# Four chunks of a spiking layer in turn, and two other stages step by step with them: the order of one hybrid kernel's front part

## The chip, the cores and the metric

The kernel runs on one NeuronCore of a Trainium2 chip. The metric is the device time of one execution in microseconds (us); the time before is the median of three runs. All engines of the core work side by side, each in the order of its own instruction stream: TensorE (PE, matrix products and transposes), VectorE (DVE), ScalarE (ACT, activation functions), GpSimd (POOL) and SyncE (SP, which here issues DMAs). An instruction waits on semaphores for what other engines produce, and everything behind it on the same engine waits with it.

## The reference

The input x has two batches of 1024 rows of 128 features, in float32. Seven blocks add to it in turn, each on a layer norm of x. The change touches how the first five are put in order:

```python
x = x + latent_attention(layernorm(x))        # 16 heads, softmax
x = x + spiking_ffn(layernorm(x))
x = x + state_space(layernorm(x))             # projections, then a scan over time
x = x + spiking_ffn(layernorm(x))
x = x + linear_attention(layernorm(x))        # a norm of its own inside
x = x + experts(layernorm(x))                 # 8 experts, summed
x = x + attention_over_batches(layernorm(x))
x = x + experts(layernorm(x))
```

with the spiking layer

```python
h = square(relu(x @ W_fc.T))                  # 128 -> 512
y = h @ W_proj.T                              # 512 -> 128
out = number_of_spikes_in_5_steps(y) / 5
```

The number of spikes grows with y, so it is computed as a count of five thresholds that y reaches.

## The kernel before

x stays on the chip as `x_res`, 16 tiles of 128 rows. A batch is 8 tiles, a *chunk* 4 tiles (512 rows), so a batch has two chunks, and chunks 0 and 1 are batch 0, 2 and 3 batch 1.

The blocks depend on each other only within a batch (until the attention over batches), so the kernel puts a part of one batch beside a part of the other. Each part is a Python generator that issues some instructions and yields: one *step*. `weave(main, side, rate)` takes a step of `main`, then as many of `side` as the rate has come due, until `main` ends; `drain` takes what is left. All of this stands in `first_layer` under a manual schedule of every engine: each engine executes in just the order in which the program issues. So the order of steps is the order of every queue. These are its stages from there on, after latent attention of batch 0:

| stage | main | side | rate |
|---|---|---|---|
| A | `into_space(0)`: spiking layer, then state space prologue, batch 0 | `row_maxima(1)` of latent attention, batch 1 | 1.25 |
| loop 0 | state space loop, batch 0 | `attend(1)`, the rest of latent attention | 1.75 |
| B | `out_of_space(0)`: second spiking layer, then linear attention, batch 0 | `into_space(1)` | 1.2 |
| loop 1 | state space loop, batch 1 | `expert_steps`, batch 0 | 1.4 |
| C | `out_of_space(1)` | the rest of `expert_steps` | 0.6 |

*The spiking layer* (`spiking_steps`) takes its chunks one after the other, in 9 steps each: statistics of the norm on DVE (L60, L61; a pair for each tile) and their root on ACT (L64); inverse and norm on DVE (L67, L71, four instructions for `f_u`); four transposes on PE (L94, `f_pt`) and a copy on ACT (L411, `f_uT`); four steps of a product (L416, `f_ph`), Relu (L418) and Square (L419) on ACT; the output product on PE (L424, `f_py`, 32 passes); and on DVE the count (L433, four times L436) and the sum into `x_res` (L439).

*The prologue* of the state space (22 steps) computes statistics and two roots, normalizes (L514, `s_u` on DVE; L517, `s_un` on ACT), transposes (L521, `s_pt`), and multiplies by the norm's weight (L522, `s_xnT`). Then come the projections, all by line 485 (`s_pm`): the input projection with the convolution, whose Silu on ACT gives `s_xc`; `wd1T`, which DVE copies to `s_rT`; the skip gates; and for each half of the features and each chunk a chain `s_z` (L555, DVE), Abs, Exp and Ln on ACT (L556 to L559), and DVE again to `s_delta` (L565) and `s_dtx` (L566). SP writes these out for the loop to load.

*Linear attention* (`linear_steps`, 13 steps) normalizes twice, `l_u` and `l_un`, each with statistics, root and eight instructions of L71 on DVE; transposes (`l_pt`, L94; `l_xnT`, L689); projects keys (`l_pm`, L695) with a maximum and an exponential, values (`l_pv`, L716) and, after transposing the keys (`l_pkt`, L725), the queries (`l_pm` again); then forms the context (`l_pc`, L734), applies it (`l_pa`, L744) and projects out (`l_po`, L750).

*Row maxima* has 49 steps: a step makes the scores of up to 512 keys for the heads of one group on PE (L223; L232 adds the mask), into three buffers `a_s`, and DVE reduces them (L241, two instructions, `a_nm`). *An expert step* (65 in all) issues two products (L799 and L800), a Silu on ACT (L802), a product on DVE (L804, `e_h`), and the output product of the step before (L823, `e_po`), which thus waits for `e_h`: a *unit*.

In stage B, eight experts' weights are loaded by SP: `load_experts`, one load for each of the first eight steps of `out_of_space(0)`.

Of the kernel before, what the change touches and what calls it, by code (L numbers as in the profile page):

```python
# [9 lines left out]
F32 = mybir.dt.float32  # L10
BF16 = mybir.dt.bfloat16
AF = mybir.ActivationFunctionType
ALU = mybir.AluOpType
# [4 lines left out]
P = 128  # L18
B = 2
L = 1024  # L20
D = 128
# [54 lines left out]
def weave(main, side, rate):  # L76

    due = 0.0
    for _ in main:
        due += rate  # L80
        while due >= 1.0:
            next(side, None)
            due -= 1.0


def drain(steps):
    for _ in steps:
        pass


def transpose4(g, ps, src):

    for t in range(4):
        g.nc.tensor.transpose(ps[:, t, :], src[:, t, :], g.ident)  # L94
# [284 lines left out]
def _fires_from(count):  # L379

    low, high = (int(np.float32(v).view(np.int32)) for v in (0.0, 2.0))
    while high - low > 1:
        mid = (low + high) // 2
        if _spikes(np.int32(mid).view(np.float32)) >= count:
            high = mid
        else:
            low = mid
    return float(np.int32(high).view(np.float32))


SPIKES_AT = [_fires_from(count) for count in range(1, 6)]


def spiking_steps(g, w, chunks, work, bank):

    nc = g.nc
    FC = 4
    for n in chunks:
        xs = g.x[:, 4 * n : 4 * n + 4, :]
        u = work.tile([P, 4, D], F32, name="f0_u")  # L400
        ln = StagedNorm(g, xs, 4, "f0")
        ln.stats(range(4))
        ln.root()
        yield
        ln.inverse()
        ln.apply(u, range(4), nc.vector)
        yield
        pt = bank("f0_pt")
        transpose4(g, pt.rearrange("p (a b) -> p a b", a=4), u)
        uT = work.tile([P, 512], F32, name="f0_uT")  # L410
        nc.scalar.copy(uT, pt)  # L411
        yield
        hT = work.tile([P, FC, 512], F32, name="f0_hT")
        for fc in range(FC):
            ph = bank("f0_ph")
            nc.tensor.matmul(ph, w["wfcT"][:, bass.ts(fc, P)], uT, start=True, stop=True)  # L416
            r = work.tile([P, 512], F32, name="f0_r", bufs=2)
            nc.scalar.activation(r, ph, AF.Relu)  # L418
            nc.scalar.activation(hT[:, fc, :], r, AF.Square)  # L419
            yield  # L420
        py = bank("f0_py")
        for t in range(4):
            for fc in range(FC):
                nc.tensor.matmul(  # L424
                    py[:, bass.ts(t, P)],
                    hT[:, fc, bass.ts(t, P)],
                    w["wprojT"][:, fc, :],
                    start=(fc == 0),
                    stop=(fc == FC - 1),
                )  # L430
        yield
        cnt = work.tile([P, 512], F32, name="f0_cnt", bufs=2)
        nc.vector.tensor_scalar(cnt, py, SPIKES_AT[0], None, ALU.is_ge)  # L433
        for level in SPIKES_AT[1:]:
            c2 = work.tile([P, 512], F32, name="f0_cnt", bufs=2)
            nc.vector.scalar_tensor_tensor(c2, py, level, cnt, ALU.is_ge, ALU.add)  # L436
            cnt = c2
        xf = xs.rearrange("p a b -> p (a b)")
        nc.vector.scalar_tensor_tensor(xf, cnt, 1.0 / 5.0, xf, ALU.mult, ALU.add)  # L439
        yield  # L440

# [391 lines left out]
class ExpertStream:  # L835
# [3 lines left out]
    NE, FC = 8, 4  # L839
# [351 lines left out]
def first_layer(g, w, open_experts, load_expert):  # L1191

    tc = g.tc

    def pool(stack, name, bufs, **kw):
        return stack.enter_context(tc.tile_pool(name=name, bufs=bufs, **kw))

    def banks(stack, name, bufs, **kw):
        ps = pool(stack, name, bufs, space=PSUM, **kw)
        return lambda tile_: ps.tile([P, 512], F32, name=tile_, tag=name)  # L1200

    right = dict(side="right")
    ends, latents, spaces = ExitStack(), ExitStack(), ExitStack()
    latent = LatentAttention(g, w, pool(latents, "a0_keep", 1, **right))
    own = pool(latents, "a0_batch1", 1, **right)
    with ExitStack() as es:
        latent.project([pool(es, "a0_batch0", 1), own])
        with tc.tile_pool(name="a0_seq", bufs=1) as seq, tc.tile_pool(name="a0_ps_a", bufs=2, space=PSUM) as ps:
            drain(latent.row_maxima(0, seq, ps, 4))
        work = pool(es, "a0_work", 2)  # L1210
        ps, ps_o = pool(es, "a0_ps_b", 3, space=PSUM), pool(es, "a0_ps_o", 1, space=PSUM)
        drain(latent.attend(0, work, ps, ps_o))

    bank = banks(spaces, "bank", 2)
    shared = StateConstants(g, w, pool(spaces, "s_one", 1))
    seq = pool(spaces, "s_seq", 2)
    dram = pool(spaces, "s_dram", 2, space=bass.MemoryType.DRAM)
    space = [StateSpace(g, w, b, shared, seq, dram) for b in range(B)]

    def into_space(b, bank, **side):  # L1220

        with tc.tile_pool(name=f"f{b}_work", bufs=1, **side) as work:
            yield from spiking_steps(g, w, [2 * b, 2 * b + 1], work, bank)
        with tc.tile_pool(name=f"s{b}_work", bufs=1, **side) as work:
            yield from space[b].prologue(work, bank)

    def out_of_space(b, bank, each_step=iter(()), **side):

        with tc.tile_pool(name=f"f{b}_work", bufs=1, **side) as work:
            for _ in spiking_steps(g, w, [2 * b, 2 * b + 1], work, bank):  # L1230
                next(each_step, None)
                yield
        with tc.tile_pool(name="l_seq", bufs=1, **side) as work:
            yield from linear_steps(g, w, b, work, bank)

    def load_experts():
        for e in range(8):
            load_expert(e)
            yield

    with tc.manual_schedule(engines=ALL):
        with (
            tc.tile_pool(name="a0_seq", bufs=1, **right) as aseq,
            tc.tile_pool(name="a0_ps_a", bufs=3, space=PSUM, **right) as ps,
        ):
            maxima = latent.row_maxima(1, aseq, ps, 2)
            weave(into_space(0, bank), maxima, 1.25)
            drain(maxima)
        work = pool(latents, "a0_work", 1, **right)
        ps, ps_o = pool(latents, "a0_ps_b", 2, space=PSUM, **right), pool(latents, "a0_ps_o", 1, space=PSUM, **right)  # L1250
        attend = latent.attend(1, work, ps, ps_o)
        with tc.tile_pool(name="s_work", bufs=1, reuse_waits="tile") as work:
            weave(space[0].loop(work, bank), attend, 1.75)
        drain(attend)
        latents.close()
        open_experts()
        with ExitStack() as es:
            bank0, bank1 = banks(es, "bank0", 3, **right), banks(es, "bank1", 3, **right)
            side = into_space(1, bank1, **right)
            weave(out_of_space(0, bank0, load_experts()), side, 1.2)  # L1260
            drain(side)
        ework = pool(ends, "e_work", 2, **right)
        ps_e, ps_o = pool(ends, "e_ps", 2, space=PSUM, **right), pool(ends, "e_ps_o", 1, space=PSUM, **right)
        experts = expert_steps(g, w, [0, 1], ework, ps_e, ps_o)
        with tc.tile_pool(name="s_work", bufs=1, reuse_waits="tile") as work:
            weave(space[1].loop(work, bank), experts, 1.4)
        spaces.close()
        with ends, ExitStack() as es:
            weave(out_of_space(1, banks(es, "bank", 3)), experts, 0.6)
            drain(experts)  # L1270


# [1 line left out]
def kernel(ctx: ExitStack, tc: tile.TileContext, d: dict, out: bass.AP):  # L1274
# [30 lines left out]
    def load_expert(e):  # L1305
        for name in ("Wg", "Wu"):
            nc.sync.dma_start(out=w[name][:, e, :], in_=d[name][e])
        nc.sync.dma_start(out=w["Wd"][:, e], in_=d["Wd"][e].rearrange("(c p) o -> p c o", p=P))

    first_layer(g, w, open_experts, load_expert)  # L1310
    layer0.close()
    experts_ffn(g, w, [2])
# [70 lines left out]
```

## Time and profile before

| what | value |
|---|---|
| median of three runs | 2337.7 us (2337.57 to 2339.66) |
| the profiled execution | 2339.02 us, its span 2337.3 us |
| PE busy | 2024.7 us, 87% of the span, 15152 instructions |
| DVE busy | 1632.9 us, 70% |
| ACT busy | 1186.0 us, 51% |
| POOL busy | 1057.0 us, 45% |
| mean granted clock of PE | 0.937 |

The stages in the profiled execution, in us from the span's start:

| stage | from | to | length |
|---|---|---|---|
| projections and latent attention of batch 0 | 0 | 312.0 | 312.0 |
| A | 312.0 | 484.3 | 172.3 |
| loop 0 | 484.3 | 691.0 | 206.7 |
| B | 691.0 | 838.6 | 147.6 |
| loop 1 | 838.6 | 1046.9 | 208.3 |
| C | 1046.9 | 1145.6 | 98.7 |
| experts, attention over batches, experts | 1145.6 | 2337.3 | 1191.7 |

How to read the profile: a line of a timeline has the start and the busy time of a group of equal instructions, the engine, the line, the operation, the tile that it writes and those that it reads, and how many; in brackets the idle time of the engine ahead of it, and whose result ended that. A line of the chain of waits has start, length, engine, tile and line. The granted clock (PEclk) is a share of full speed.

### The profile page before, as it was taken

What the parts mean: (1) busy time and instruction counts of PE and PEld (TensorE: products, weight loads), DVE (VectorE), ACT (ScalarE), POOL (GpSimd) and SP (SyncE); (2) the same over time, 40 slices, a digit from 0 to 9 for tenths busy, and PEclk for the clock granted to TensorE, in tenths of its full rate; (3) what the DMA queues carried; (4) which work ended last, traced back from release to release, by engine and by line L of the source; (5) the groups of instructions that cost most, each with busy time, mean ns of one, the idle gap of its engine ahead of it and who ended that gap; (6) DMA issues with size and microseconds to landing.
All of it is one profiled execution on the core that took longest, in us unless ns stands there. A gap on an engine that the chain in (4) does not pass through costs nothing.

```text
span 2337.3 us, 36191 instructions
## 1 busy us (share of the span) xinstructions
PE 2024.7 (87%) x15152; PEld 1189.1 (51%) x15152; DVE 1632.9 (70%) x1988; ACT 1186.0 (51%) x1488; POOL 1057.0 (45%) x588
## 2 busy tenths in 40 slices
PE   7679988887986848788898898999977999999999
PEld 4223344223334413234446576777745777777764
DVE  5941057788874569984423798989977989898832
ACT  1024521254633468754322676777734777677722
POOL 0011100042310000100102599999999999999910
PEclk9989988878988879999899999999999999999999
DMA  3000000086741068630000000000000000000000
GB/s 86 1 1 1 1 1 1 18 205 155 179 111 55 19 163 189 158 83 0 1 1 1 1 1 2 1 2 1 2 6 1 2 2 1 2 6 1 2 5 5
DMA packets 35779, 85.92 MB, mean 37 GB/s; under 512 B 4960, under 2 KB 15648, under 8 KB 35488
## 3 DMA queue, kind: packets, MB, share of 16 engines
q1 hardware_dynamic: 35152, 82.28, 14.4%
q8 instruction: 119, 1.95, 0.4%
q10 hardware_dynamic: 464, 1.33, 0.3%
q14 instruction: 44, 0.36, 0.1%
HBM read 78.35 MB, written 5.24 MB: 36 GB/s over the span
## 4 chain that ended last, share of the span: by engine, by line
PE 41%; POOL 13%; DVE 10%; issue 3%; ACT 3%; DMA 1%; SPq 0%; DVEq 0%; ACTq 0%; POOLq 0%
PE h_pd L1062 7%; POOL h_a L1072 7%; PE e_pgu L877 6%; POOL h_e L1056 5%; PE h_pd L903 4%; PE h_s L1028 4%; PE e_pg L799 4%; PE h_po L1078 4%; PE e_po L823 4%; PE e_pu L800 3%; DVE s_h L636 2%; PE s_pm L485 1%; DVE e_h L804 1%; DVE s_h L635 1%; DVE h_m L1039 1%
## 5 line engine op out<-in xcount | busy, mean ns | idle before, releaser
L1072 POOL TENSOR_TENSOR h_a<-h_e,h_r 128x2048 f32<-128x2048 f32 x128 | 581.2, 4541 | 0.0
L1039 DVE TENSOR_REDUCE h_m<-h_s 128x128 f32<-128x2048 f32 x128 | 293.3, 2291 | 74.8 <-PE h_s L1028 74.6
L1056 POOL TENSOR_TENSOR h_e<-h_e 128x512 f32<-128x512 f32 x256 | 318.4, 1261 | 46.8 <-ACT h_e L1048 46.8
L1062 PE MATMUL h_pd<-h_e,ident 128*128 128x128 f32 x2048 | 279.7, 291 | 44.0 <-POOL h_e L1056 33.0
L1062 PEld LDWEIGHTS h_pd<-h_e,ident 128*128 128x128 f32 x2048 | 253.3, 200 | 96.9 <-POOL h_e L1056 77.4
L1048 ACT ACTIVATE h_e<-h_e 128x1024 f32<-128x1024 f32 x256 | 256.6, 1049 | 81.7 <-DVE h_e L1045 80.6
L1045 DVE TENSOR_TENSOR h_e<-h_s,h_m 128x2048 f32<-128x2048 f32 x128 | 292.6, 2286 | 2.7
L302 POOL TENSOR_SCALAR_AFFINE_SELECT a_pT<-a_pT 128x256 f32<-128x256 f32 x128 | 97.2, 774 | 428.6 <-ACT a_pT L299 427.7
L299 ACT ACTIVATE a_pT<-a_st 128x1024 f32<-128x1024 f32 (+1 forms) x192 | 145.2, 808 | 140.4 <-PE a_st L289 138.3
L884 ACT ACT_TABLE_LOAD x106 | 136.0, 1283 | 153.0 <-PE e_pgu L877 152.3
L804 DVE TENSOR_TENSOR e_h<-e_sg,e_pu 128x512 f32<-128x512 f32 x128 | 86.9, 685 | 177.0 <-PE e_pu L800 151.7
L241 DVE TENSOR_REDUCE a_nm<-a_s 128x2 f32<-128x1024 f32 (+7 forms) x144 | 168.1, 1218 | 44.4 <-PE a_s L232 24.0
L823 PE MATMUL e_po<-e_h,Wd 128*128 128x512 f32 x256 | 138.6, 627 | 40.4 <-DVE e_h L804 40.2
L802 ACT ACTIVATE e_sg<-e_pg 128x512 f32<-128x512 f32 x128 | 76.0, 596 | 189.7 <-PE e_pg L799 189.4
L903 PEld LDWEIGHTS h_pd<-Wd,e_h 128*128 128x128 f32 x1024 | 125.6, 191 | 90.5 <-DVE e_h L892 79.8
L223 PE MATMUL a_s<-a_latT,a_qT 32*128 32x512 f32 (+3 forms) x768 | 121.0, 606 | 53.6 <-DVE a_nm L241 52.0
L877 PE MATMUL e_pgu<-e_uT,Wg 128*128 128x256 f32 x512 | 154.3, 383 | 4.0 <-ACT h_qz L992 2.1
L903 PE MATMUL h_pd<-Wd,e_h 128*128 128x128 f32 x1024 | 149.2, 288 | 5.8 <-DVE e_h L892 3.6
L1028 PE MATMUL h_s<-h_qz,h_kT 32*128 32x512 f32 x1024 | 147.0, 644 | 8.1 <-DVE h_e L1045 7.0
L877 PE MATMUL e_pgu<-e_uT,Wu 128*128 128x256 f32 x512 | 152.4, 379 | 0.0
L636 DVE TENSOR_TENSOR_SCAN s_h<-s_a,s_h 128x1024 f32<-128x1024 f32 x64 | 147.3, 2302 | 5.9 <-ACT s_a L604 1.6
L1048 ACT ACT_TABLE_LOAD x107 | 137.3, 1283 | 26.0 <-DVE h_e L1045 21.0
(246 smaller groups left out, 3190.2 us busy)
## 6 DMA issues: line engine op xcount, KB each, us to landing
s_a<-s_steps SPq DMA_DIRECT2D x64, 512.0 KB, 4.8
s_h<-s_steps SPq DMA_DIRECT2D x64, 512.0 KB, 6.4
s_steps<-s_delta SPq DMA_DIRECT2D x4, 512.0 KB, 2.6
s_steps<-s_dtx SPq DMA_DIRECT2D x4, 512.0 KB, 3.3
Wg<-in_Wg_dram SPq DMA_DIRECT2D x8, 256.0 KB, 6.0
Wu<-in_Wu_dram SPq DMA_DIRECT2D x8, 256.0 KB, 5.9
Wd<-in_Wd_dram SPq DMA_DIRECT2D x8, 256.0 KB, 6.1
x_res<-in_x_dram SPq DMA_DIRECT2D x4, 256.0 KB, 7.9
```

The lines of the kernel that those rows point to most:

```text
L241: nc.vector.tensor_reduce(nm[:, half, i, h : h + together], s[:, :, :n], AX.X, ALU.max, negate=True)
L636: nc.vector.tensor_tensor_scan(h, a, h, 0.0, ALU.mult, ALU.add)
L823: nc.tensor.matmul(po, w["Wd"][:, e, fc, :], hp, start=(e == 0 and fc == 0), stop=last)
L877: nc.tensor.matmul(pgu[:, k, :], w[name][:, e, f], uT, start=True, stop=True)
L903: nc.tensor.matmul(po[:, t, :], h[:, bass.ts(t, P)], self.w["Wd"][:, e, fc, :], start=(k == 0), stop=(k == 1))
L1028: nc.tensor.matmul(s[:, j, :].rearrange("p (k q) -> p k q", k=K), kTs[b][quad, bass.ts(kb, P)], qzs[b][quad, :, bass.ts(qb, P)], start=Tru ...
L1039: nc.vector.tensor_reduce(m, heads.rearrange("p h q -> p q h"), AX.X, ALU.max)
L1045: nc.vector.tensor_sub(e, heads, m.unsqueeze(1).to_broadcast([P, H, P]))
L1048: nc.scalar.activation(eh, eh, AF.Exp, scale=scale)
L1056: nc.gpsimd.tensor_add(e2[:, 4 * half : 4 * half + 4, :], e[:, h0 : h0 + 4, :], e[:, h0 + 4 : h0 + 8, :])
L1062: nc.tensor.matmul(pd, g.ident, e2[:, k, :], start=(k == 0), stop=(k == 7))
L1072: nc.gpsimd.tensor_mul(a, e, r.unsqueeze(1).to_broadcast([P, H, P]))
```

## The change

`spiking_steps` takes one chunk instead of a list, with buffers that are named for the chunk's parity, and `merge` takes a step of each of several streams in turn. The two chunks of a batch's spiking layer become two streams that alternate, in `into_space` and `out_of_space` alike, so these have 9 rounds for it in place of 18 steps (31 and 22 steps in all, before 40 and 31). In stage B, `into_space(1)` and `out_of_space(0)` alternate too, in place of the weave at 1.2: so the four chunks go step by step in turn, and then a step of the prologue of batch 1 and a step of linear attention of batch 0, until linear attention ends. The rates in A and C become 1.6 and 0.8. Relu writes into `f0_hT` and Square works in place.

```diff
+def merge(*streams):
+    streams = list(streams)
+    done = object()
+    while streams:
+        streams = [stream for stream in streams if next(stream, done) is not done]
+        if streams:
+            yield
...
-def spiking_steps(g, w, chunks, work, bank):
+def spiking_steps(g, w, n, work, bank):
     nc = g.nc
     FC = 4
-    for n in chunks:
-        xs = g.x[:, 4 * n : 4 * n + 4, :]
-        u = work.tile([P, 4, D], F32, name="f0_u")
-        ln = StagedNorm(g, xs, 4, "f0")
...
-        uT = work.tile([P, 512], F32, name="f0_uT")
...
-        hT = work.tile([P, FC, 512], F32, name="f0_hT")
...
-            r = work.tile([P, 512], F32, name="f0_r", bufs=2)
-            nc.scalar.activation(r, ph, AF.Relu)
-            nc.scalar.activation(hT[:, fc, :], r, AF.Square)
...
-            c2 = work.tile([P, 512], F32, name="f0_cnt", bufs=2)
+    tile_ = lambda name, tag: work.tile([P, 512], F32, name=name, tag=f"{tag}{n % 2}")
+    xs = g.x[:, 4 * n : 4 * n + 4, :]
+    u = tile_("f0_u", "f0_a").rearrange("p (a b) -> p a b", a=4)
+    ln = StagedNorm(g, xs, 4, f"f{n}")
...
+    uT = tile_("f0_uT", "f0_b")
...
+    hT = work.tile([P, FC, 512], F32, name=f"f0_hT{n % 2}")
...
+        nc.scalar.activation(hT[:, fc, :], ph, AF.Relu)
+        nc.scalar.activation(hT[:, fc, :], hT[:, fc, :], AF.Square)
...
+        c2 = tile_("f0_cnt", "f0_a" if k % 2 else "f0_b")
...
 def into_space(b, bank, **side):
-            yield from spiking_steps(g, w, [2 * b, 2 * b + 1], work, bank)
+            yield from merge(*[spiking_steps(g, w, n, work, bank) for n in (2 * b, 2 * b + 1)])
...
 def out_of_space(b, bank, each_step=iter(()), **side):
-            for _ in spiking_steps(g, w, [2 * b, 2 * b + 1], work, bank):
+            for _ in merge(*[spiking_steps(g, w, n, work, bank) for n in (2 * b, 2 * b + 1)]):
                 next(each_step, None)
                 yield
...
-            weave(into_space(0, bank), maxima, 1.25)
+            weave(into_space(0, bank), maxima, 1.6)
...
-            side = into_space(1, bank1, **right)
-            weave(out_of_space(0, bank0, load_experts()), side, 1.2)
-            drain(side)
+            drain(merge(into_space(1, bank1, **right), out_of_space(0, bank0, load_experts())))
...
-            weave(out_of_space(1, banks(es, "bank", 3)), experts, 0.6)
+            weave(out_of_space(1, banks(es, "bank", 3)), experts, 0.8)
```

More of the change, by code (lines that the diff above doesn't have):

```diff
@@ L391 @@
 SPIKES_AT = [_fires_from(count) for count in range(1, 6)]
-def spiking_steps(g, w, chunks, work, bank):
+def spiking_steps(g, w, n, work, bank):
     nc = g.nc
     FC = 4
-    for n in chunks:
-        xs = g.x[:, 4 * n : 4 * n + 4, :]
-        u = work.tile([P, 4, D], F32, name="f0_u")
-        ln = StagedNorm(g, xs, 4, "f0")
-        ln.stats(range(4))
-        ln.root()
-        yield
[L405 to L409, printed above, removed]
-        uT = work.tile([P, 512], F32, name="f0_uT")
-        nc.scalar.copy(uT, pt)
-        yield
-        hT = work.tile([P, FC, 512], F32, name="f0_hT")
-        for fc in range(FC):
-            ph = bank("f0_ph")
-            nc.tensor.matmul(ph, w["wfcT"][:, bass.ts(fc, P)], uT, start=True, stop=True)
-            r = work.tile([P, 512], F32, name="f0_r", bufs=2)
-            nc.scalar.activation(r, ph, AF.Relu)
-            nc.scalar.activation(hT[:, fc, :], r, AF.Square)
[L420 to L434, printed above, removed]
-            c2 = work.tile([P, 512], F32, name="f0_cnt", bufs=2)
[L436 to L440, printed above, removed]
@@ new lines, in spiking_steps @@
+    tile_ = lambda name, tag: work.tile([P, 512], F32, name=name, tag=f"{tag}{n % 2}")
+    xs = g.x[:, 4 * n : 4 * n + 4, :]
+    u = tile_("f0_u", "f0_a").rearrange("p (a b) -> p a b", a=4)
+    ln = StagedNorm(g, xs, 4, f"f{n}")
+    ln.stats(range(4))
+    ln.root()
+    yield
+    ln.inverse()
+    ln.apply(u, range(4), nc.vector)
+    yield
+    pt = bank("f0_pt")
+    transpose4(g, pt.rearrange("p (a b) -> p a b", a=4), u)
+    uT = tile_("f0_uT", "f0_b")
+    nc.scalar.copy(uT, pt)
+    yield
@@ new lines, in spiking_steps @@
+    hT = work.tile([P, FC, 512], F32, name=f"f0_hT{n % 2}")
+    for fc in range(FC):
+        ph = bank("f0_ph")
+        nc.tensor.matmul(ph, w["wfcT"][:, bass.ts(fc, P)], uT, start=True, stop=True)
+        nc.scalar.activation(hT[:, fc, :], ph, AF.Relu)
+        nc.scalar.activation(hT[:, fc, :], hT[:, fc, :], AF.Square)
+        yield
+    py = bank("f0_py")
+    for t in range(4):
+        for fc in range(FC):
+            nc.tensor.matmul(
+                py[:, bass.ts(t, P)],
+                hT[:, fc, bass.ts(t, P)],
+                w["wprojT"][:, fc, :],
+                start=(fc == 0),
+                stop=(fc == FC - 1),
+            )
@@ L451 @@
+    yield
+    cnt = tile_("f0_cnt", "f0_a")
+    nc.vector.tensor_scalar(cnt, py, SPIKES_AT[0], None, ALU.is_ge)
+    for k, level in enumerate(SPIKES_AT[1:]):
+        c2 = tile_("f0_cnt", "f0_a" if k % 2 else "f0_b")
+        nc.vector.scalar_tensor_tensor(c2, py, level, cnt, ALU.is_ge, ALU.add)
+        cnt = c2
+    xf = xs.rearrange("p a b -> p (a b)")
+    nc.vector.scalar_tensor_tensor(xf, cnt, 1.0 / 5.0, xf, ALU.mult, ALU.add)
+    yield
 class StateConstants:
```

## The prediction

> **What bounds the kernel now.** I read the table of windows first, cut at the borders of the stages: the change touches three stretches, and everything between and after them keeps its instructions.
>
> ```profile
> core 0: us, PE busy (x) PEld busy (x) DVE busy (x) ACT busy (x) POOL busy (x), PEclk, DMA share, GB/s
> 312.00:484.30 172.30, 146.29 (x722) 64.86 (x720) 127.03 (x199) 44.34 (x64) 3.24 (x2) 0.82 0.07 20
> 691.00:838.60 147.60, 95.80 (x376) 54.74 (x368) 75.64 (x206) 61.29 (x98) 7.33 (x4) 0.81 0.21 66
> 1046.90:1145.60 98.70, 83.89 (x299) 45.02 (x297) 45.40 (x125) 39.99 (x61) 3.64 (x3) 0.95 0.00 0
> ```
>
> Column two is the length. I call the three A (172.3 us), B (147.6) and C (98.7): 418.6 of 2337.3 us, 18%. PE has the most busy time in each, but stands idle for 26.0, 51.8 and 14.8 us, and its granted clock is 0.82, 0.81 and 0.95. So no engine is full: what sets each end is a chain that goes round PE, DVE and ACT. Next the engines' timelines, for where the chain breaks. In A, PE's:
>
> ```profile
> 343.74 1.65 PE L223 MATMUL a_s<-a_latT,a_qT 32*128 32x384 f32 x4 [3.87 <-DVE a_nm L241]
> 378.71 2.08 PE L223 MATMUL a_s<-a_latT,a_qT 32*128 32x512 f32 x8 [3.43 <-DVE a_nm L241]
> 462.26 2.08 PE L223 MATMUL a_s<-a_latT,a_qT 32*128 32x512 f32 x4 [4.27 <-DVE a_nm L241]
> ```
>
> The bracket is the idle time before and its releaser. PE waits for a score buffer while DVE counts spikes, and then works at half pace (at 462.26 four passes take 2.08 us; at 374.15, 1.13). In B, PE's timeline, DVE's, and the chain of waits:
>
> ```profile
> 731.88 1.24 PE L94 MATMUL f_pt<-ident,f_u 128*128 128x128 f32 x4 [8.69 <-DVE f_u L71]
> 761.60 1.35 PE L521 MATMUL s_pt<-ident,s_un 128*128 128x128 f32 x4 [8.64 <-ACT s_un L517]
> 767.59 11.52 PE L485 MATMUL s_pm<-s_xnT,s_inw 128*128 128x512 f32 x24
> ...
> 719.65 0.69 DVE L433 TENSOR_SCALAR f_cnt<-f_py 128x512 f32<-128x512 f32 x1 [13.67 <-PE f_py L424]
> 747.62 0.69 DVE L433 TENSOR_SCALAR f_cnt<-f_py 128x512 f32<-128x512 f32 x1 [13.79 <-PE f_py L424]
> ...
> 793.85 0.76 DVE s_z L555
> 829.73 0.70 DVE s_dtx L566
> ```
>
> DVE idles twice for 13.7 us, once for each pair of chunks; then the state space prologue runs to its last s_dtx at 830.43. In C, PE's:
>
> ```profile
> 1109.93 2.08 PE L823 MATMUL e_po<-e_h,Wd 128*128 128x512 f32 x2 [6.07 <-DVE e_h L804]
> 1118.36 2.07 PE L823 MATMUL e_po<-e_h,Wd 128*128 128x512 f32 x2 [3.37 <-DVE e_h L804]
> 1120.23 1.55 PE L94 MATMUL l_pt<-ident,l_un 128*128 128x128 f32 x8
> ```
>
> Linear attention's two norms run while PE has only two expert units to do; between 1103.6 and 1120.2 PE works 7.16 of 16.6 us.
>
> **What the change costs.** No arithmetic is added or taken away. Per chunk there stay 4 Relu and Square pairs on ACT (0.58 + 0.63, pitch 1.15), 32 output passes on PE (3.57 together) and a count block on DVE (4.24: six instructions, the first at 719.65, the next block's at 723.89). The new buffers, and the square written in place, cost nothing: ACT already runs the two in turn, at the same 1.15. POOL's and SP's instructions keep their order; the expert weights that SP loads beside B are first used in the loop after 838.6, which is their cover. ACT loses two table loads in C (2 x 1.28).
>
> *A.* Both chunks' steps come as 9 rounds that carry 14 maxima steps (18 steps and 22 before); the prologue's 22 rounds carry 35 (before 27). The two output blocks come together (7.1 us on PE, where DVE waits: before 3.52 and 3.81), and so do the count blocks (8.5 us on DVE, where PE waits: before 3.87 and 3.43). That is a wash but for one restart fewer: a window cut at 343.7 to 352.0, just behind the first wait, has a clock of 0.50. It costs PE 4 us, of which I count 2, since DVE is busy for 7.57 of these 8.3 us anyway. Eight maxima steps move behind: five of 1024 columns (2.36) and three of 256 (0.75) make 14.1 us of DVE. So the prologue's statistics, at 378.9 before, start near 378.9 - 14.1 - 2 = 363. From 378.9 to 480.4, behind the last maximum, DVE was busy 76.8 of 101.5 us: it idled 24.7. If the steps fill idle time only, the stretch stays 101.5 and A gains 16; if they fill none, it grows by 14.1 and A gains 2. I choose near the second: each step needs its PE part too, about 10 us in all at that part's clock of 0.77, and DVE's waits there are single ones of up to 3.4 us, which a step of 2.36 fills only in part. **-4, between -12 and +3** (one new wait of 3.87 with its cold restart, against the saved one).
>
> *B.* All four chunks' statistics (4 x 1.6) end at 706.5 and the norms at 711.9. ACT then sets the pace: 16 pairs x 1.15 = 18.4 from 713.3, so 731.7 (its order puts the four copies of uT ahead of the first Relu). The first count comes at 731.5, four blocks of 4.24 end at 748.5; before, the last ended at 760.77, with the prologue's statistics already done (4.9 us). Behind it DVE now has, in its order: prologue statistics 3.2, linear's 3.2, l_u 2.1 to 4.2 (both lengths are in its rows), four s_u 1.1, linear's second statistics 3.2, s_xnT 0.7, s_u 1.1, l_un 2.1: 16.7 to 18.8, plus waits for ACT's roots of some 2, about 20: 768.5. PE's order puts l_pt (1.1) ahead of the first s_pm (before: after 24 passes of it), so the projections wait for linear's whole norm: 769.6, against 767.59. Queued behind that wait are all the projections, and for those wait ACT's s_xc and DVE's s_z. Before the first s_z PE also does l_pkt (0.96), the q part of l_pm (0.86) and more of l_pc, so 26.3 becomes 28.4: s_z at 798.0, 4 us later. What follows is shorter: the third s_z waited until 815.45 for linear's blocks on PE, and now the four chains come back to back: 8.7 + 0.7 + 3 x 7.5 (a chain from 822.98 to 830.42) = 31.9, to 829.9 against 830.4. PE's gap grows to 18 us (742 to 760), for which I add 1.5 of restart. **+1, between -6 and +6**: the lower end is the front's gain of 12.3 less half of the norms, the upper one the 4 us at s_z kept, and 2 more.
>
> On that gap: the rows show s_pm's first two passes at 0.85 each (0.43 later) after waits of 8.64 and 3.49, and full pace from 769.9: a price of 0.9 us. [...]
>
> *C.* Here 22 steps x 0.8 = 17.6 expert steps go between, against 31 x 0.6 = 18.6. Linear attention's statistics start near 1090 (1103.64 before): nine rounds hold 7.2 unit steps, the 18 before 10.8, and 3.6 steps of 2.58 and one output block's wait make 13.6. Thirteen linear steps then carry 10.4 units instead of 7.8. PE's waits through the two norms, 6.07 + 3.37 = 9.4, become about 5.5 (1.3 + 3.7 + 0.5: the two added units cover 2.58 each, less what they wait for e_h themselves); l_pt stands near 1104.5. Then PE's work is as before, three units more behind l_pt (7.7). I get the end 7.7 earlier by this order, and 5.4 by PE's idle time alone (14.2 to 8.8), to which the half pace after the gaps adds about 2 (2.08, 1.92, 1.49 and 2.07 for blocks of 1.02). **-6.5, between -10 and -1.**
>
> Sum: -4 + 1 - 6.5 = -9.5. The profiled execution took 2339.0 (span 2337.3, 1.7 around it), 1.3 above the median of the runs, 2337.7; from that median the forecast is **2328**.
>
> **Rivals.** *B keeps its front.* The counts end 12 us earlier, and if linear's norm on DVE hides in waits for roots and transposes, 9 of it stay: -4 - 9 - 6.5, about 2318. For it: DVE idles 27 us at 691 to 748. Against: l_pt ahead of s_pm in PE's order. Chance 0.22.
>
> *The gains dissolve.* In A the moved steps cost what they save, in C the units only change places, since PE's work (83.9 of 98.7) is the same: 0 + 0 to 1 and -3, about 2335. For it: the wait of 2.4 to 4.3 us for a_nm appears anywhere in A. Against: C's two large holes have a known filler. Chance 0.18.
>
> *Half clock through B's projections.* After 18 us of idle, PE meets transposes, and then work broken by short waits. Each us of the 28.4 up to s_z that runs at half clock costs another, and the last chain moves with it: slower than before by what can be told from 9.5 + 4.7 = 14.2 us on. Two thirds of it at half make 2328 + 19 = 2347. For it: in A, windows at 462 to 480 have 0.50 throughout after a wait of only 4.27, and s_pm x4 took 3.72 there. Against: at 767.59 the clock recovered within 2.3 us of dense work. Chance 0.12.
>
> **How the numbers follow.** 4.7 us (0.2%) is what a measurement can tell from no change. The forecast has 0.48, and alone a range of 2320 to 2334. Faster: 0.48 less 0.03 for its upper edge, 0.22, and 0.04 of the third case (2330 to 2343): 0.71. Same: that 0.03, and 0.12 of the third, 0.15. Slower: 0.12, and 0.02 of the third, 0.14. The range goes from 2314 (the second case with A at -8) to 2341: left out are most of the slow case and a little below, under 2 in 10.
>
> **What would show it.** A: the two count blocks adjacent near 347 to 355, the last a_nm near 476. B: first f_cnt near 731.5 less A's gain, all times there shifted alike; l_pt ahead of s_pm; s_z 28 us after s_pm's start (26.3 before); the last s_dtx 139 us into the stage. C: largest wait at e_po below 4, l_pt 15 earlier, the stage some 92. The loops (206.7 and 208.3) and the last 1191.7 us unchanged. Wrong would be a clock below 0.6 in B's projections, or DVE idle in A's prologue part still above 24.

## The result, and the profile after

| | before | after |
|---|---|---|
| median | 2338.5 us (2331.0 to 2341.8, 6 runs) | 2350.5 us (2344.6 to 2356.3, 6 runs) |
| ratio | | 1.006, interval 1.0042 to 1.0078 |
| profiled execution, its span | 2339.0, 2337.3 us | 2351.9, 2350.2 us |

The change made the kernel 12 us slower. The forecast was 9.5 us faster, with a range of 2314 to 2341 us; the result lies above it.

The windows of the changed kernel, cut at the borders of its own stages (columns as before: length, busy times, the granted clock):

```profile
313.95:498.10 184.15, 155.65 (x722) 68.72 (x720) 127.68 (x198) 42.52 (x63) 3.23 (x2) 0.78 0.06 20
704.40:852.00 147.60, 92.56 (x376) 52.62 (x368) 75.32 (x207) 61.18 (x98) 7.30 (x4) 0.80 0.21 67
1058.60:1159.80 101.20, 85.83 (x299) 46.30 (x297) 45.83 (x131) 37.55 (x59) 3.63 (x2) 0.93 0.00 0
```

A is 11.9 us longer, B is equal, C is 2.5 longer. In A the same 722 instructions keep PE busy 9.4 us longer (155.65 for 146.29) at a clock of 0.78 for 0.82, and its idle time grows by 2.5. So most of the loss is pace, not waiting. The clock's record is 1.00 or 0.50 throughout (37 stretches of each in before's trace, 39 in the changed kernel's); from A's first a_s to its first s_h PE works 48.9 us at half clock before and 69.3 after. By an estimate these 20.4 us more cost half of it, 10.2 (four passes take 2.08 us there in place of 1.13); 7 of them lie ahead of the first s_pm of the prologue (22.2 and 29.4), 13 behind it (26.7 and 40.0), where the prologue also carries the moved maxima steps. PE's timeline of the changed kernel shows the first of these stretches:

```profile
344.18 7.36 PE L433 MATMUL f_py<-wprojT,f_hT 128*128 128x128 f32 x64
...
355.06 1.13 PE L233 MATMUL a_s<-a_latT,a_qT 32*128 32x512 f32 x4
364.27 2.08 PE L233 MATMUL a_s<-a_latT,a_qT 32*128 32x512 f32 x4 [8.09 <-DVE a_nm L251]
...
393.49 4.96 PE L494 MATMUL s_pm<-s_xnT,s_inw 128*128 128x512 f32 x8
```

and DVE's, at the same place:

```profile
352.65 1.82 DVE L251 TENSOR_REDUCE a_nm<-a_s 128x2 f32<-128x768 f32 x2 [6.56 <-PE a_s L242]
354.39 0.68 DVE L442 TENSOR_SCALAR f_cnt<-f_py 128x512 f32<-128x512 f32 x1
...
363.00 2.35 DVE L251 TENSOR_REDUCE a_nm<-a_s 128x2 f32<-128x1024 f32 x2
```

The output products of both chunks stand end to end on PE (7.36 us, in which DVE idles 6.56), and then both count blocks on DVE (354.39 to 363.0, in which PE idles 8.09). Behind the hole four passes take 2.08 us in place of 1.13, and the full pace comes back only at 396.2, inside the projections that begin at 393.49. The windows there have the clock in the third column from the right:

```profile
364.20:380.00 15.80, 14.14 (x44) 5.05 (x44) 12.36 (x29) 0.60 (x2) 0.00 (x0) 0.50 0.01 2
380.00:400.00 20.00, 18.06 (x76) 8.82 (x76) 12.31 (x24) 4.53 (x10) 3.23 (x2) 0.60 0.00 0
```

For all runs below, the stages are measured between instructions that every kernel has: A from the first a_s of batch 1 to the first s_h, B from the first s_po of batch 0 to the last s_dtx, C from the last s_po of batch 1 to the last l_po. By that measure before has 167.4, 137.5 and 92.6, the changed kernel 179.2, 137.4 and 95.1. In three kernels whose C is issued as before (b_only, b_lead3, b_lead9), C still took 94.6 to 94.7 instead of 92.6, so 2 us of it mean nothing: in b_only PE idles 13.5 us there, just as before, but works 12.8 us at half clock in place of 7.4. What stands ahead of A and behind C is never edited and scatters from run to run, by up to 8 and 5 us, which is why the stages tell more than the totals.

### The profile page after: what moved, and what is told of

The parts are those of the page before. It is cut to its first block, busy times and chain, and to the rows that moved or that the text cites. A ratio compares the mean times of both kernels' runs of the same rounds, so it can differ in the third digit from the quotient of the medians.

```text
span 2350.2 us, 36194 instructions
## 1 busy us (share of the span) xinstructions
PE 2037.6 (87%) x15152; PEld 1192.3 (51%) x15152; DVE 1632.7 (69%) x1988; ACT 1182.8 (50%) x1486; POOL 1058.7 (45%) x588
## 3 DMA queue, kind: packets, MB, share of 16 engines
HBM read 78.35 MB, written 5.24 MB: 36 GB/s over the span
## 4 chain that ended last, share of the span: by engine, by line
PE 39%; POOL 14%; DVE 11%; issue 3%; ACT 3%; DMA 1%; SPq 0%; DVEq 0%; ACTq 0%; POOLq 0%
POOL h_a L1081 7%; PE h_pd L1071 7%; PE e_pgu L886 6%; POOL h_e L1065 6%; PE h_pd L912 4%; PE h_s L1037 4%; PE e_pg L808 4%; PE h_po L1087 4%; PE e_pu L809 3%; PE e_po L832 3%; DVE s_h L645 2%; DVE s_h L644 1%; DVE e_h L813 1%; DVE h_m L1048 1%; POOL e_u L71 1%
## 5 line engine op out<-in xcount | busy, mean ns | idle before, releaser
L1065 POOL TENSOR_TENSOR h_e<-h_e 128x512 f32<-128x512 f32 x256 | 323.6, 1302 | 46.8 <-ACT h_e L1057 46.8
L309 ACT ACTIVATE a_pT<-a_st 128x1024 f32<-128x1024 f32 (+1 forms) x192 | 145.2, 808 | 140.9 <-PE a_st L299 138.8
L233 PE MATMUL a_s<-a_latT,a_qT 32*128 32x512 f32 (+3 forms) x768 | 134.2, 661 | 52.0 <-DVE a_nm L251 50.7
```

The lines of the kernel that those rows point to most:

```text
L1065: nc.gpsimd.tensor_add(e2[:, 4 * half : 4 * half + 4, :], e[:, h0 : h0 + 4, :], e[:, h0 + 4 : h0 + 8, :])
```

## The experiments

All are the changed kernel's text with one stage or more set back or edited; a stage that is not named has the order of before (with the new buffers, which cost nothing: A takes 167.4 in b_only too).

**Each stage alone.** The edit in A's run; B's and C's likewise:

```diff
-            weave(out_of_space(1, banks(es, "bank", 3)), experts, 0.8)
+            weave(out_of_space(1, banks(es, "bank", 3), False), experts, 0.6)
```

with `False` for chunks one after the other, and stage B woven at 1.2 as before.

> The kernel before, with the change in stage A alone (alternating chunks and the rate of 1.6); B and C in the order of before. If the loss is A's own, A takes 183 to 185 us (172.3 before, 184.2 after) and the total is 9 to 14 us above before; B (147.6) and C (98.7) keep their lengths within 2 us. If the loss of the changed kernel is spread over the stages or comes from how they act on each other, the total is less than 6 us above before.

> The kernel before, with the change in stage B alone (four chunks in turn, then prologue and linear attention in turn). By the two traces the stretch from the first s_po to the last s_dtx is equal (137.5 before, 137.4 after): total within 4 us of before, or up to 2 us below it. If B's part of the change pays when A does not disturb it, 4 us or more below before.

> The kernel before, with the change in stage C alone (alternating chunks and the rate of 0.8). If C's loss is its own, from the first s_po of batch 1 to the last l_po it takes 2 to 3 us more than before, with holes of about 5, 2 and 5.5 us at e_po. If it was brought on by an earlier stage, C is 5 us or more shorter, as was forecast (6.5).

| run | median, ratio (interval) | A | B | C |
|---|---|---|---|---|
| a_only | 2351.2, 1.0068 (1.0047 to 1.0089) | 179.3 | 136.3 | 92.6 |
| b_only | 2339.2, 1.0019 (1.0006 to 1.0032) | 167.4 | 138.8 | 94.7 |
| c_only | 2336.1, 1.0003 (0.9988 to 1.0017) | 167.2 | 137.6 | 94.9 |

A alone has the whole loss: its A is as long as the changed kernel's, and its total is 16.3 us above that of before (2334.8 in this comparison), a little more than the 9 to 14 expected. b_only is 4.4 above, just outside the 4 expected; its loop 1 is 1.7 longer than before and its unedited C 2.1. C's change alone can't be told from none, since 94.9 is a length that an unedited C nearly shows too: what has to be explained there is the missing gain of 6.5.

**Is it the moved steps?** `weave_at` takes a rate for each step of its first stream.

```diff
-            weave(into_space(0, bank), maxima, 1.6)
+            weave_at(into_space(0, bank, True), maxima, [22 / 9 + 1e-6] * 9 + [27 / 22 + 1e-6] * 23)
```

> As the run with A alone, but the nine rounds of the spiking layer carry 22 maxima steps, as many as the 18 steps did before, and the 22 prologue steps 27: no maxima step moves behind, only the chunks alternate. Theory 1, that two count blocks end to end are what costs (8.5 us of DVE, a hole of about 8 us on PE, half clock behind it): the hole of 7 us or more stays, and A takes 178 us or more. Theory 2, that the eight moved steps cost it, at about 3 us each in the prologue: A is back at 172 within 2 us, total within 4 us of before.

Median 2352.5, ratio 1.0071 (1.0051 to 1.0091), A 179.6. With no step moved, A costs the same. The front (to the prologue's first statistics) took 67.3 us for 61.9 before, the prologue's part 108.5 for 101.6. That speaks against theory 2, though not cleanly: this run has a stretch of its own of some 13.6 us at half clock ahead of the blocks (the last section), which alone can cost up to 6.8, an estimate (half of it). PE's timeline has the hole again:

```profile
362.76 7.41 PE L450 MATMUL f_py<-wprojT,f_hT 128*128 128x128 f32 x64
...
383.38 2.50 PE L250 MATMUL a_s<-a_latT,a_qT 32*128 32x512 f32 x12 [7.81 <-DVE a_nm L268]
```

**Taking the blocks apart.** Once by yielding within the count, once by letting the second chunk follow two rounds later:

```diff
+        if pieces and k in (0, 2):
+            yield
```
```diff
+        first, second = streams
+        return merge(first, (None for part in (range(2), second) for _ in part))
```

> Stage A as changed (alternating chunks), but each count block is yielded in three pieces of two instructions, so that row maxima come between them on DVE; 33 steps at a rate of 1.5, B and C in the order of before. Measured from the first a_s to the first s_h, A is 167.4 before and 179.2 after. Theory 1 (two count blocks end to end starve PE, and the half clock behind the hole is most of the price): no hole over 4 us at the counts, A 167 within 3. Rival (alternating costs for another reason: products and output blocks of two chunks together, the norms together): the hole goes, but A stays at 176 or more.

> Stage A with alternating chunks, the second chunk two rounds behind the first, so that output blocks and count blocks of the two are apart again; 33 steps at 1.5, B and C in the order of before. Theory 1: two holes of about 4 us as in before in place of one of 8; A 166 to 171. Rival (the alternation itself): 176 or more.

> The kernel before, chunks one after the other, with the count blocks yielded in three pieces in A alone, rate 1.125 over 44 steps in place of 1.25 over 40. If a hole of 3.9 us behind a count block costs A its cold stretch, the two holes shrink below 2.5 and A falls by 4 to 8 us, to 160 to 163; if idle time only moves elsewhere, A stays at 167 within 2.

| run | median, ratio (interval) | A |
|---|---|---|
| a_split | 2348.6, 1.0066 (1.0044 to 1.0087) | 171.8 |
| a_stagger | 2342.0, 1.0028 (1.0015 to 1.0041) | 169.2 |
| a_fine_seq | 2335.9, 0.9998 (0.9986 to 1.0011) | 166.5 |

With the second chunk two rounds behind, A is within 1.8 us of before, and 10 of the 11.9 us are gone, though the chunks still alternate and 33 of the 49 maxima steps stand beside the prologue or behind (27 before, 35 as changed). So neither the alternation as such nor the moved steps make the price, at most 1.8 us of it in this trace; what the two chunks do end to end does. The stagger takes norms and products apart too, so it doesn't single out the blocks of counts. And the total is still 6.1 us above its before (2336.0), of which A shows 1.8: the other 4 are not explained. In A's window PE is busy 148.0 us at a clock of 0.81, near before's. PE's timeline of a_stagger: there is one hole, half as long, as each is in before.

```profile
347.07 3.79 PE L443 MATMUL f_py<-wprojT,f_hT 128*128 128x128 f32 x32
...
358.71 1.13 PE L243 MATMUL a_s<-a_latT,a_qT 32*128 32x512 f32 x4
363.88 2.07 PE L243 MATMUL a_s<-a_latT,a_qT 32*128 32x512 f32 x8 [4.04 <-DVE a_nm L261]
```

Splitting the counts is less clear. In its profiled execution A recovered 7.4 us, between what the two theories gave, but loop 0 behind it took 210.0 for 207.5, the total stayed at 1.0066, and that execution was the fastest of six (2345.0); how much it recovers as a rule stays open. On the order of before the split brought 0.9 us in A, not the 4 to 8 of the first theory.

In both runs the holes shrank, and the half clock didn't shrink with them (a_split 61.0 us for 69.3 as changed, a_fine_seq 55.5 for 48.9 before). First a_split, then a_fine_seq, whose waits at the two count blocks were 3.87 and 3.43 before:

```profile
354.85 2.06 PE L240 MATMUL a_s<-a_latT,a_qT 32*128 32x512 f32 x4 [2.27 <-DVE a_nm L258]
```
```profile
339.56 1.12 PE L240 MATMUL a_s<-a_latT,a_qT 32*128 32x384 f32 x4 [1.04 <-DVE a_nm L258]
...
378.89 0.80 PE L240 MATMUL a_s<-a_latT,a_qT 32*128 32x128 f32 x4 [1.66 <-DVE a_nm L258]
```

In a_split the hole of 8.09 has become 2.27, yet the half clock lasts there from 354.9 to 389.1, 34 us, where the changed kernel has 32 behind its hole (364.3 to 396.2). The six traces of A, with the busy time of PE split by the granted clock:

| run | A | PE busy at half clock | PE idle |
|---|---|---|---|
| before | 167.4 | 48.9 | 25.6 |
| changed | 179.2 | 69.3 | 28.1 |
| a_same_count | 179.6 | 64.5 | 29.7 |
| a_split | 171.8 | 61.0 | 23.2 |
| a_stagger | 169.2 | 50.4 | 25.0 |
| a_fine_seq | 166.5 | 55.5 | 22.4 |

A is half of the third column, plus the fourth, plus 116 to 119 us in every row, PE's work at full pace. With the blocks apart the half pace is nearly back to before's; with the counts cut into pieces PE idles less, but much of the half pace stays.

**What makes C's holes.** First the blocks in smaller pieces (the statistics are shown; the counts and the application of the norm are cut likewise), then ACT's root out of the way of the units' Silu:

```diff
-        ln.stats(range(TPB))
-        ln.root()
+        ln.stats(range(4))
+        if pieces:
+            yield
+        ln.stats(range(4, TPB))
+        ln.root()
```
```diff
         ln.stats(range(TPB))
-        ln.root()
+        if not late:
+            ln.root()
         yield
+        if late:
+            ln.root()
```

> The kernel before, with stage C's count blocks in three pieces and linear attention's two norms in four steps each, rate 0.477 over 39 steps in place of 0.6 over 31, so as many expert steps. From the last s_po to the last l_po C is 92.6 before. If a block of count and statistics ahead of e_h on DVE is what makes the holes of 6.07 and 3.37 us, they shrink below 3 each, and C is 86 to 90; if they wait for ACT, C stays within 1.5.

> The kernel before, with one change in stage C: the root of each of linear attention's norms is issued on ACT after the expert steps that follow the statistics, not ahead of them, two expert steps follow each statistics and one each application, 0.55 per step of the spiking layer, none or few behind. If the holes at e_po (6.07 and 3.37) come from ACT, whose Silu for a unit stands behind the root that waits for DVE's statistics, they shrink below 2.5 each and C, 92.6 from the last s_po to the last l_po, is 86 to 89. If DVE's own block of count and statistics is enough to make them, C stays at 91 or more.

C stayed at 92.9 (median 2337.7, ratio 1.0011, 0.9999 to 1.0022) with the pieces, and rose to 95.8 (2341.6, 1.0022, 1.0011 to 1.0034) with the later root. In both the alternative without a gain came true: for the pieces the one that says the holes wait for ACT, for the later root the one that says DVE's block is enough. The traces show how both can be. ACT's timeline of c_fine_seq:

```profile
1102.24 0.30 ACT L64 ACTIVATE l_rs<-l_mv,eps 128x8 f32<-128x8 f32 x1 [5.06 <-DVE l_mv L61]
1102.56 1.28 ACT L826 ACT_TABLE_LOAD   x1
1103.86 1.08 ACT L826 ACTIVATE e_sg<-e_pg 128x512 f32<-128x512 f32 x2
```

The Silu of two units stands behind the root in ACT's order, and the root waits 5.06 us for all of DVE's statistics, in pieces or not. The two holes at e_po shrank, but only to 3.97 and 1.91, and waits of 2.61 (for f_u) and 1.13 (for l_ctx) came elsewhere: PE idles 13.6 us in C, as before (13.5). With the later root, PE's timeline of c_root has no hole in the second norm, but two others; below them ACT's, ahead of the first:

```profile
1083.44 1.67 PE L852 MATMUL e_po<-e_h,Wd 128*128 128x512 f32 x2 [4.49 <-DVE e_h L833]
...
1112.58 2.08 PE L852 MATMUL e_po<-e_h,Wd 128*128 128x512 f32 x2 [3.70 <-DVE e_h L833]
```
```profile
1080.46 0.30 ACT L64 ACTIVATE f_rs<-f_mv,eps 128x4 f32<-128x4 f32 x1 [5.58 <-DVE f_mv L61]
1080.77 1.28 ACT L831 ACT_TABLE_LOAD   x1
1082.07 1.08 ACT L831 ACTIVATE e_sg<-e_pg 128x512 f32<-128x512 f32 x2
```

The first is again ACT's: behind the first chunk's count, the second chunk's own root, which the edit did not move, waits for its statistics, and the units' Silu behind the root. The second is DVE's: e_h comes directly behind the second count block and linear attention's statistics, without idle time. So both engines make holes; this run also has other rates, so which unit falls behind which block changed with it.

**The same cure in C.** The second chunk two rounds behind, 0.736 in place of 0.8:

> The kernel before, with stage C as changed except that the second chunk of the spiking layer runs two rounds behind the first; 0.736 per step, as many expert steps as with 0.8. C, from the last s_po to the last l_po, is 92.6 before and 94.9 with C's change alone. Theory 1 (two count blocks end to end ahead of e_h, a hole of 4.8 us and half clock behind it): the first hole falls below 2.5 and C is 92.6 or less. Rival (the rate, which puts seven units among the first steps and three more behind l_pt): C stays at 94 or more.

Median 2327.8, ratio 0.9976 (0.9960 to 0.9992), C 86.8: 5.8 us less than before, 8.1 less than with C's change alone. PE's timelines, first c_only, then c_stagger:

```profile
1093.90 2.07 PE L839 MATMUL e_po<-e_h,Wd 128*128 128x512 f32 x2 [4.75 <-DVE e_h L820]
1100.04 1.12 PE L839 MATMUL e_po<-e_h,Wd 128*128 128x512 f32 x2 [1.83 <-DVE e_h L820]
1108.47 2.07 PE L839 MATMUL e_po<-e_h,Wd 128*128 128x512 f32 x2 [5.59 <-DVE e_h L820]
```
```profile
1087.45 1.12 PE L842 MATMUL e_po<-e_h,Wd 128*128 128x512 f32 x2 [0.90 <-DVE e_h L823]
1093.98 2.07 PE L842 MATMUL e_po<-e_h,Wd 128*128 128x512 f32 x2 [3.69 <-DVE e_h L823]
1100.12 1.14 PE L842 MATMUL e_po<-e_h,Wd 128*128 128x512 f32 x2 [0.65 <-DVE e_h L823]
```

12.2 us of holes become 5.2. As many expert steps go between in all (about eight instead of seven beside the spiking layer), so the rate is hardly what withheld the gain.

**Where B's front went.** Linear attention begins some rounds behind the prologue:

```diff
+        for _ in range(lead):
+            yield
         with tc.tile_pool(name="l_seq", bufs=1, **side) as work:
```

> The kernel before, with stage B as changed (four chunks in turn), but linear attention of batch 0 begins five rounds after the prologue of batch 1, so that the prologue's norm is ahead of linear's on DVE and the first s_pm ahead of l_pt on PE. Measured from the first s_po to the last s_dtx, B is 137.5 before and 137.4 as changed. If the front's 12 us are given back because the projections wait for linear's whole norm (17 us of idle PE ahead of s_pt), s_pm starts 7 to 9 us earlier and B is 126 to 131. If the front is paid back by the chains behind s_z or by cold projections, B is 135 or more.

> As b_lead5, with linear attention nine rounds behind, so that all eight blocks of the input projection are issued before linear's norms. If only the norm's place on DVE and of l_pt on PE mattered, B as with five rounds within 2 us; if PE's linear blocks then fall among the four chains of s_z, as they do before (third s_z at 815.45 waiting for PE), B is 2 to 5 us longer than with five.

> The kernel before, with stage B as changed and linear attention three rounds behind the prologue (0 gave 137.4, 5 gave 125.8, 9 gave 130.7 from the first s_po to the last s_dtx). If each round by which linear's norm stands ahead of the prologue's on DVE costs its share, B is 128 to 133; if only the place of l_pt against the first s_pm counted, it is 126 within 1.

| rounds behind | median, ratio (interval) | B | loop 1 to the last s_po |
|---|---|---|---|
| 0 (b_only) | 2339.2, 1.0019 (1.0006 to 1.0032) | 138.8 | 223.3 |
| 3 | 2323.3, 0.9953 (0.9939 to 0.9967) | 125.4 | 223.1 |
| 5 | 2328.6, 0.9963 (0.9947 to 0.9979) | 125.8 | 222.8 |
| 9 | 2344.6, 1.0034 (1.0017 to 1.0050) | 130.7 | 231.4 |

PE's timeline, first of the changed kernel, then of b_lead5:

```profile
772.24 1.36 PE L530 MATMUL s_pt<-ident,s_un 128*128 128x128 f32 x4 [17.07 <-ACT s_un L526]
...
780.39 1.76 PE L104 MATMUL l_pt<-ident,l_un 128*128 128x128 f32 x6 [1.59 <-DVE l_un L71]
781.94 5.24 PE L494 MATMUL s_pm<-s_xnT,s_inw 128*128 128x512 f32 x8
```
```profile
757.39 1.36 PE L537 MATMUL s_pt<-ident,s_un 128*128 128x128 f32 x4 [12.16 <-ACT s_un L533]
760.28 1.35 PE L537 MATMUL s_pt<-ident,s_un 128*128 128x128 f32 x4 [1.53 <-ACT s_un L533]
761.43 15.62 PE L501 MATMUL s_pm<-s_xnT,s_inw 128*128 128x512 f32 x32
```

Counted from the first s_po (705.6 and 694.2), the projections begin after 76.3 and 67.2 us, 9.1 sooner, and 32 passes follow each other where 8 did. Three rounds are as good as five, so it is the place of linear's norm ahead of the projections that counts, not its share round by round. At nine rounds linear's blocks wait for DVE and ACT among the chains of s_z, and end only in the loop, which takes 231.4 us for 221.7 before.

**Together.**

> Three edits together on the order of before: count blocks in three pieces in A (chunks one after the other), stage B as changed with linear attention five rounds behind, and the later root in C. If the stages add, about -1 in A, -8 in B and -5 in C: 14 us below before, ratio near 0.994. If a gain in one stage is given back in the next, the ratio is above 0.997.

> The changed kernel in all three stages, with three corrections: the second chunk two rounds behind in A (rate 1.5) and in C (0.736), and linear attention five rounds behind in B. If the stages add: A 169.2, B 125.8, C 92 to 93 against 167.4, 137.5 and 92.6 before, so 9 to 10 us below before and a ratio of 0.996; the changed kernel had 1.006. If a stage gives back what an earlier one gained, above 0.998.

> The kernel before, with count blocks in three pieces in A (chunks one after the other) and stage B as changed with linear attention five rounds behind; C as before. If the stages add: A 166.4, B 124, C 92.6, so 13 to 14 us below before, a ratio of 0.9945.

> What gained in each stage, together: in A the order of before with count blocks in three pieces, in B the change with linear attention five rounds behind, in C the change with the second chunk two rounds behind. If the stages add: A 166.4, B 124.1, C 86.8 against 167.4, 137.5 and 92.6 before, and 1 us more in loop 1: 19 us below before, a ratio of 0.992. If the last gain is given back behind C, above 0.994.

| run | median, ratio (interval) | A | B | C |
|---|---|---|---|---|
| best1 | 2328.3, 0.9964 (0.9952 to 0.9976) | 166.3 | 124.0 | 95.9 |
| mended | 2319.5, 0.9939 (0.9919 to 0.9959) | 170.9 | 124.0 | 86.7 |
| best2 | 2325.0, 0.9952 (0.9936 to 0.9969) | 166.6 | 124.1 | 92.6 |
| best3 | 2316.2, 0.9931 (0.9918 to 0.9945) | 166.3 | 124.0 | 86.4 |

Each stage keeps within 2 us the length that it had alone (A of one and the same order takes 169.2 in a_stagger and 170.9 in `mended`); best1's C is c_root's, whose loss was not known when best1 was forecast. The totals follow the sums less closely. In medians best1, best2 and best3 are 7, 10 and 16.5 us below before, where 14, 13 to 14 and 19 were forecast, and `mended` 16, where 9 to 10 were. `mended` is the changed kernel with three corrections that only move whole blocks, which take it from 12 us above before to 16 below. The fastest, best3, keeps A's order of before. Against before its stages give -1.1, -13.5 and -6.2, 4 us more than the total shows.

## Why the prediction was wrong

**A is the step that failed.** Of the 21.5 us between the forecast and the result A has 15.9 (-4 forecast, +11.9 measured) and C 9.0. The text put two output blocks and two count blocks end to end and called it "a wash but for one restart fewer". The lengths were right (8.5 us of counts forecast, 8.6 measured), the price was not: the sum compared one long hole with two short ones by their length, and took the clock behind them for a fee of some us for each restart. What was measured is the whole time that PE works at half pace: 20.4 us more of it (10.2 lost) and 2.5 more idle. a_same_count shows the same loss with no step moved (though with a stretch of its own at half clock), and a_stagger shows 10 us of it gone with the blocks apart. Why the half pace lasts longer in this order stays open: it is not the length of the hole alone, since a_split, whose hole is 2.27 us, has 61.0 us of it for 69.3, and a_fine_seq, with holes of 1.04 and 1.66, has 55.5, more than before's 48.9.

**The bounds of the moved steps failed with it.** Eight steps were to cost between 0 and 14.1 us, by DVE's durations. The front did become shorter (50.0 us for 61.9; 16 were forecast), but the prologue's part grew by 24.2 (125.8 for 101.6), 3.0 per step. DVE is busy there for 14.1 us more, just what was counted, but its idle time grew too, by 10, from 24.7 to 34.7, where the bound took it to stay at most as it was; above 24 was the text's own sign of being wrong. In the stretch at half clock DVE's reductions of 1024 columns start 3.7 us apart (363.00, 366.71), not 2.36: there PE, not DVE, sets a step's cost. The bound should have been taken from PE's rows at half pace, where four passes take 2.08.

**B was right to about a us in its places.** Less the 13.4 us by which its stage begins later, s_pm stood at 768.5 (forecast 769.6), the first s_z at 798.9 (798.0), the end at -0.1 us (+1). Two errors offset each other on the way: s_z came 30.4 us behind s_pm, not 28.4, and the chains behind it were shorter. The 1.5 us of restart in its sum was an estimate that no run shows: in the rows of before it is 0.9, behind 8.64 and 3.49 us of idle, and the changed kernel has 1.6 behind 17.07, 3.43 and 1.59 (s_pm x8 in 5.24 us for 3.60). That the front's gain was eaten by linear's norm ahead of the projections was argued; b_lead5 shows it, with 11.6 us returned when that norm is put behind. So the rival "B keeps its front" was false for this order, and its price of 9 a fair estimate of what another order has.

**C's term failed too.** It was to give -6.5, between -10 and -1, and gave +2.5, of which 2 mean nothing. Linear's statistics were to begin 13.6 us sooner and did by some 5.8 (1109.5 against 1103.64, less the later stage of 11.7): the two count blocks end to end, ahead of the statistics, made a hole of 4.76 there; the other 3 us of the difference were not traced. The holes were to be 5.5 and were 4.76, 1.70 and 5.59; for the last two the text overlooked ACT, where a unit's Silu stands behind the root. c_stagger comes near the forecast (5.8 for 6.5, with 5.2 us of holes), but with the blocks apart, so for an order that the text did not have. The text counted 13 steps of linear attention; there are 14, which moves 18.6 and 17.6 to 19.2 and 18.4 and changes nothing.

**The slow rival had its half clock in the wrong stage.** It was priced for B's projections, up to 28 us. There 17 us of idle cost 1.6 (s_pm x8 in 5.24 for 3.60). The row it leaned on was A's own (462 to 480, a clock of 0.50), and A is where PE worked at half clock for 69.3 us (before 48.9). The rival that the gains dissolve named A's bad case too, but as zero.

## What to carry to other kernels

When two streams alternate step by step, their blocks of one kind come end to end on one engine: check the longest block in every engine's order against the buffers of whoever waits behind it, and let the second stream follow a few steps later. Don't price a hole on PE by its length: ahead of B's projections 17 us of idle cost 1.6 here (s_pm x8 in 5.24 us for 3.60); ahead of A's maxima PE worked 28.6 us at half pace behind 8.09 us of idle, which cost 14, half of it, as an estimate, and the half pace stayed about as long (34 us for 32) when the hole was cut to 2.27. Where a gain is to come from a front, look which block of the other stream stands ahead of the first instruction that needs it.

## What the runs showed of the hardware

Two waits of one length went with unlike stretches at half clock. In the changed kernel a wait of 1.97 us early in A, the only one of over 0.4 in its window, is followed by some 3.6 us at half clock; in a_same_count one of 1.96, again the only one, goes with some 13.6, though only one maxima step more stands ahead of it. (The lengths are twice the missing share of the clock times the window's length.) The waits, and the windows that hold them, first of the changed kernel, then of a_same_count:

```profile
323.31 0.49 PE L233 MATMUL a_s<-a_latT,a_qT 32*128 32x128 f32 x4 [1.97 <-DVE a_nm L251]
```
```profile
314.00:343.90 29.90, 27.37 (x186) 15.20 (x184) 17.97 (x44) 10.84 (x19) 0.00 (x0) 0.94 0.00 1
```
```profile
325.54 0.80 PE L250 MATMUL a_s<-a_latT,a_qT 32*128 32x128 f32 x4 [1.96 <-DVE a_nm L268]
```
```profile
319.87:360.00 40.13, 37.68 (x212) 17.75 (x212) 25.16 (x42) 10.95 (x19) 0.00 (x0) 0.83 0.00 1
```

In one place the drop shows only after the wait is over: in the changed kernel a wait of 3.26 us is followed by one group at full pace (the clock is 1.00 from 439.44 to 440.48), and the next is at half (0.50 from 440.49 to 442.50).

```profile
439.44 1.13 PE L233 MATMUL a_s<-a_latT,a_qT 32*128 32x512 f32 x4 [3.26 <-DVE a_nm L251]
440.49 2.07 PE L494 MATMUL s_pm<-s_rT,wd2T 64*128 64x512 f32 x2
```

What decides how long the half clock lasts at a given wait was not tried.
